# A four-layer graph kernel on one core: later places for a feature sum and for the gates' products, and a last row tile in two column halves

## The chip, the cores and the metric

The kernel runs on one core of one Trainium2 chip. The metric is the device time of one execution in microseconds; the time before is 2896.17 us, the median of three runs (2895.42 to 2900.82). A run with the hardware profiler gives, beside its own time, a record of each instruction: its engine, its start, its duration and the semaphores it waited for. The engines are called as the profile calls them: PE is TensorE's matrix product, PEld its loads of the stationary operand, DVE is VectorE, ACT is ScalarE, POOL is GpSimd, and SP is SyncE, which issues most loads.

## The reference, cut to what matters

There are 2708 nodes with 512 features, and an adjacency of 2708 x 2708, all in fp32. Each of four layers computes a new feature matrix, adds it to the old one and normalizes the rows.

```python
deg = jnp.maximum((adj != 0).astype(jnp.float32).sum(-1), 1.0)
x = _layernorm(x + _L0_gnn_ref(x, adj), axis=-1)
x = _layernorm(x + _L1_gnn_ref(x, adj, adj, ...), axis=-1)      # attention and two gates
x = _layernorm(x + _L2_gnn_ref(x, adj, L2_gnn_weight), axis=-1) # three hops, p = adj @ p
x = _layernorm(x + _L3_gnn_ref(x, adj, deg[..., None], L3_gnn_W, L3_gnn_b), axis=-1)

# layer 1, the gates
type_sum_a = adj_a @ x
type_sum_b = adj_b @ x
attn_a = sigmoid(concatenate([type_sum_a, x], axis=1) @ Wa.T + ba)
attn_b = sigmoid(concatenate([type_sum_b, x], axis=1) @ Wb.T + bb)
# ...
return sigmoid(attn_a * x_a + attn_b * x_b)

# layer 3, the last
a_norm = dinv * (adjacency + eye(n)) * dinv                     # dinv = node_degree ** -0.5
pooled = a_norm @ x + x
return relu(pooled @ W + b)
```

Here `node_degree` is the same shape as a column, so that the kernel can put both factors into one reciprocal per row and a diagonal that it adds to the adjacency.

## The kernel before

The kernel doesn't write its instructions in the order of the program. It collects functions in a list, each with a position, sorts the list and calls them; within one engine the recorded order then follows the list closely, though not exactly, since a scheduler has the last word. So a larger number in `at(...)` is a later place in the queues of the engines, and nothing else.

```python
    def at(pos, fn, hold=False):
        # ...
        events.append((pos, len(events), go if hold else fn))

    S = [28.0 * s for s in range(8)]          # where each sweep over the adjacency starts
    # ...
    for p, _, fn in sorted(events, key=lambda e: e[:2]):
        fn()
```

Products of large matrices are split into seven smaller ones by sums of quarter blocks (the scheme of Strassen and Winograd). Layer 1 has one level of it: per range of up to 384 rows there are seven sub-products of ten row tiles each, one list unit for each sub-product. Its results lie in C, whose halves are h = 1 and h = 0. From C come the gates: `pg` is four products of C with the padded gate weights, ScalarE copies it to `zg`, and `pz` takes from it two columns per row tile.

```python
    def done1(p0, dp, last, R0, n, h, C, tiles):
        Z = {}

        def gates():

            pg = bank("pg")
            for c in range(DC):
                nc.tensor.matmul(pg[32 * c : 32 * c + 32, :n], wab_pad[:, c, :], C[h, c][:, :n], start=True, stop=True)
            Z[0] = trans("zg")
            nc.scalar.copy(Z[0][:, :n], pg[:, :n])

        def gate_tile(i, t, lo, w):
            # ... pz<-pick,zg on TensorE, a sum on VectorE, a sigmoid on ScalarE

        at(p0 + 0.05, gates)
        for i, (t, lo, w) in enumerate(tiles):
            def b(i=i, t=t, lo=lo, w=w):
                gate_tile(i, t, lo, w)
                if not last:
                    return
                # ... last range: the dense product of this row tile, ps_d
            at(p0 + 0.25 + (dp * i if last else 0.02 * i), b)
        if last or h:
            return

        Y = {}
        at(p0 + 0.3, lambda: Y.update(row_sums({(i, c): C[1 - i, c] for i in range(2) for c in range(DC)}, n)))
        # ... seven(...) from p0 + 0.6 on: the dense products (ps) of these sums
```

`row_sums` writes some of its sums in place, over halves of C that `pg` reads. The degrees of the nodes are counted on the way: VectorE adds masks in `deg` (L974), and `ds` (L988) sums it by columns with 128x1 products. The scores of the attention are VectorE's work too (L911).

Layer 3, like the hops, has two levels. A range g has seven outer products, two list units each, and each outer product seven sub-products, `u = 2 / 7` units each. The moving operands `z` are blocks of the adjacency, loaded and combined in place (L1231) or corrected on the diagonal (L1245); the stationary ones are blocks `b11` to `b22` of the features and four sums of them, `t1` to `t4` (L1265).

```python
                def tsum(nm, x, y, T=T, st=st, nk=nk):
                    for i in range(2):
                        # ...
                        T[nm, i] = ring_tile("t")
                        nc.vector.tensor_tensor(get(nm), get(x), get(y), ALU.subtract)

                for nm, x, y, pos in (("t3", "b22", "b12", -0.9), ("t1", "b12", "b11", 0.1), ("t2", "b22", "t1", 0.9),
                                      ("t4", "b21", "t2", 1.9)):
                    if g == j == 0:
                        pos = max(pos, 0.4)
                    at(b + u * pos, lambda a=(nm, x, y), f=tsum: f(*a))
                # ...
                for i, (v, z, home, start) in enumerate((
                        ("b11", (0, 0), "u", 1), ("t3", "s3", "c", 1), ("t1", (1, 0), "d", 1), ("t2", (0, 0), "u", 0),
                        ("t4", (1, 1), "c", 0), ("b22", (0, 0), "d", 0), ("b21", (0, 1), "a", 1))):
                    for k in range(nk):
                        at(b + u * (i + k / nk), lambda a=(i, v, z, home, start, k), f=step: f(*a))
```

So `t3` of outer product j stands 0.9 of a sub-product ahead of it, and is first read by its second sub-product. In layer 3 the feature blocks B11 (group tiles B11A to B11D) come from the rows X3 that layer 2 writes just before; they serve the third outer product, j = 2 of g = 0.

The end of the kernel is six row tiles, of 128, 128, 83, 128, 128 and 83 rows, each finished by itself:

```python
            def b(s=s, lo=lo, w=w, r0=r0, got=got):
                px = dense(lambda c: cc(s, c)[:, lo : lo + w], W[6], w)
                r = 12 * g + 6 * h + 3 * s + lo // P
                nc.vector.scalar_tensor_tensor(px[:w], px[:w], rdeg_f[:w, r : r + 1], vec[6][:w], ALU.mult, ALU.add)
                finish(s, lo, w, got["x"], px)

            p = p0 - 0.095 + 0.14 * i
            at(p - 0.6, a)
            at(p, b)
```

`dense` is four products with all 512 columns, into one PSUM bank. `finish` takes the relu and adds the old row (L1491), lets `layernorm` compute the statistics (L557, L559, L561 on VectorE, a power of -1/2 on GpSimd at L562, L564 on VectorE), normalizes the 512 columns on ScalarE (L567) and stores the tile. The four steps after the product follow each other, each waiting for the one before.

Of the kernel before, what the change touches and what calls it, by code (L numbers as in the profile page):

```python
# [21 lines left out]
F32 = mybir.dt.float32  # L22
BF = mybir.dt.bfloat16
AF = mybir.ActivationFunctionType
ALU = mybir.AluOpType
P = 128
EPS = 1e-5
NH = 1354
# [40 lines left out]
def gnn_kernel(ctx: ExitStack, tc: tile.TileContext, x, adjT, w_sa, a_sa, w_gcn, b_gcn, wab, bab, w_hop, w_out,  # L69
               b_out, out):  # L70
    nc = tc.nc
    N, D = x.shape
    NT = 2 * KT
    DC = D // P
    HD = D // 2
# [94 lines left out]
    def bank(nm, shape=None):  # L170
        return psum.tile(shape or [P, D], F32, name=nm, tag="x", bufs=8)
# [6 lines left out]
    def at(pos, fn, hold=False):  # L178

        def go():  # L180
            n = len(nc.cur_bb.bb.instructions)
            fn()
            held.update(range(n, len(nc.cur_bb.bb.instructions)))

        events.append((pos, len(events), go if hold else fn))
# [819 lines left out]
# [12 lines that stand above are left out]
            if i == 0:  # L1017
                Z[1] = bank("pz", [P, 8])
            pz = Z[1][:, 2 * i : 2 * i + 2]
            nc.tensor.matmul(pz[:w], Z[0][:, lo : lo + w], pick, start=i == 0, stop=True, skip_group_check=True)  # L1020
            nc.vector.tensor_tensor(gate[:w, t, :], pz[:w], gate_x[:w, t, :], ALU.add)
            nc.scalar.activation(gate[:w, t, :], gate[:w, t, :], AF.Sigmoid)

        def finish(t, w, y):
            nc.scalar.mul(y[:w], y[:w], gate[:w, t, 1:2])
            move(nc.gpsimd, XB[t], y[:w])

        at(p0 + 0.05, gates)
        for i, (t, lo, w) in enumerate(tiles):
            def b(i=i, t=t, lo=lo, w=w):  # L1030
                gate_tile(i, t, lo, w)
                if not last:
                    return
                px = dense(lambda c: C[h, c][:, lo : lo + w], W[1], w)
                y = nat("y")
                nc.vector.tensor_tensor(y[:w], px[:w], vec[1][:w], ALU.add)
                finish(t, w, y)

            at(p0 + 0.25 + (dp * i if last else 0.02 * i), b)
        if last or h:  # L1040
            return

# [3 lines that stand above are left out]
            H, y = {}, []  # L1046

            def b7(part, t=t, lo=lo, w=w, H=H, y=y):
                if part == 0:
                    y.extend(nat("y") for _ in range(2))  # L1050
                seven(part, Y, W[8], H, lo, w, y, None, [vec[1], vec[1]])
                if part == 1:
                    for j in range(2):
                        finish(t + KT * (1 - j), w, y[j])

            at(p0 + 0.6 + 0.56 * i, lambda f=b7: f(0))
            at(p0 + 0.6 + 0.56 * i + 0.26, lambda f=b7: f(1))
# [142 lines left out]
    def sweep2(base, ext, done, on_diag=False):  # L1200
        nk = K2 + ext
        u = 2 / 7
        for g, (i0, n) in enumerate(RANGES2):
            Q, C = {}, {}
            for j, m in enumerate(ORDER2[g]):
# [61 lines left out]
                for nm, x, y, pos in (("t3", "b22", "b12", -0.9), ("t1", "b12", "b11", 0.1), ("t2", "b22", "t1", 0.9),  # L1267
                                      ("t4", "b21", "t2", 1.9)):
                    if g == j == 0:
                        pos = max(pos, 0.4)  # L1270
                    at(b + u * pos, lambda a=(nm, x, y), f=tsum: f(*a))

                def stat(v, k, T=T, st=st):
# [212 lines left out]
    def done6(p0, dp, g, i0, n, h, cc, tiles):  # L1486
# [12 lines left out]
        for i, (s, lo, w) in enumerate(tiles[:3] if not end else ()):  # L1499
# [7 lines left out]
            def b(part, lo=lo, w=w, got=got, z=z, H=H, r=r):  # L1507
                if part == 0:
                    z.extend(nat("z") for _ in range(2))
                seven(part, Y, W[7], H, lo, w, z, [rdeg_f[:w, r + 3 * s : r + 3 * s + 1] for s in range(2)],  # L1510
                      [vec[6], vec[6]])
                if part == 1:
                    for s in range(2):
                        finish(s, lo, w, got[s], z[s])
# [5 lines left out]
        for i, (s, lo, w) in enumerate(tiles[3:] + tiles[:3] if end else ()):  # L1520
            got = {}
            r0 = i0 + s * n + lo

            def a(r0=r0, w=w, got=got):
                got["x"] = fetch2(X3, h, r0, w)

            def b(s=s, lo=lo, w=w, r0=r0, got=got):
                px = dense(lambda c: cc(s, c)[:, lo : lo + w], W[6], w)
                r = 12 * g + 6 * h + 3 * s + lo // P
                nc.vector.scalar_tensor_tensor(px[:w], px[:w], rdeg_f[:w, r : r + 1], vec[6][:w], ALU.mult, ALU.add)  # L1530
                finish(s, lo, w, got["x"], px)

            p = p0 - 0.095 + 0.14 * i
            at(p - 0.6, a)
            at(p, b)

    sweep2(S[6], 0, done6, True)

# [54 lines left out]
```

## Time and profile before

| | |
|---|---|
| time, median of 3 runs | 2896.17 us (2895.42 to 2900.82) |
| span of the profiled run | 2892.7 us, granted TensorE clock 0.996 |
| TensorE, matrix product | 2839.9 us busy, 98% |
| TensorE, weight loads | 1871.5 us, 65% |
| VectorE | 2269.3 us, 78% |
| ScalarE | 569.2 us, 20% |
| GpSimd | 618.2 us, 21% |
| moved between HBM and the core | 511.52 MB, 177 GB/s on average |

The busy time of an engine counts what it executes, not its waits. "Idle before" in a line is the time that the engine stood before that instruction, with what ended the wait. One fp32 product of the program shows as two records of TensorE; ends of neighbouring records overlap a little, so that a group's length is its span and not a sum. Layer 1 lies between about 435 and 890 us, the products of layer 3 from about 2485 us to the end.

### The profile page before, as it was taken

How to read it: one execution, taken by the hardware profiler on the slowest of the kernel's cores; microseconds unless marked ns; L12 is line 12 of the kernel's file. 1: busy time of each engine (PE TensorE's matmuls, PEld its weight loads, DVE VectorE, ACT ScalarE, POOL GpSimd, SP SyncE). 2: the span in 40 equal slices, each digit the busy share in tenths (PEclk: the TensorE clock that was granted, in tenths of full speed). 3: DMA queues.
4: the chain of work that ended last, by engine and by line, in shares of the span. 5: the costliest groups of instructions: out<-in, count | busy, mean ns of one | idle time of the engine just before them, and what ended most of it. 6: DMA issues, size and time to landing. Idle time of an engine off the chain costs nothing. (4 is left out here: it accounts for less than half of the span.)

```text
span 2892.7 us, 37709 instructions
## 1 busy us (share of the span) xinstructions
PE 2839.9 (98%) x10955; PEld 1871.5 (65%) x10955; DVE 2269.3 (78%) x5875; ACT 569.2 (20%) x1122; POOL 618.2 (21%) x1119
## 2 busy tenths in 40 slices
PE   7999999999999999999999999999999999999998
PEld 6655665657765656866666666666666666666665
DVE  6998698576748775775699787887878878799987
ACT  4554200101136554542100000000000100100001
POOL 0223223123320101122213133031330211501202
PEclk9999999999999999999999999999999999999999
DMA  7666466354544433565677767566675665754552
GB/s 231 201 199 187 134 203 221 116 174 144 178 148 125 123 117 98 154 196 158 192 206 232 214 193 242 172 203 200 197 238 172 189 195 173 236 161 145 175 142 90
DMA packets 373455, 511.52 MB, mean 177 GB/s; under 512 B 63722, under 2 KB 326628, under 8 KB 373248
## 3 DMA queue, kind: packets, MB, share of 16 engines
q1 hardware_dynamic: 307128, 372.01, 44.0%
q0 software_dynamic: 49536, 126.39, 12.8%
q10 hardware_dynamic: 16584, 10.71, 1.3%
q8 instruction: 87, 1.43, 0.2%
q14 instruction: 120, 0.98, 0.1%
HBM read 425.22 MB, written 83.67 MB: 176 GB/s over the span
## 5 line engine op out<-in xcount | busy, mean ns | idle before, releaser
L1231 DVE TENSOR_TENSOR z<-z 128x339 f32<-128x339 f32 (+1 forms) x966 | 453.9, 502 | 13.9 <-PE accu L1284 4.0
L1302 ACT COPY q<-accu 128x338 f32<-128x338 f32 (+1 forms) x84 | 34.5, 442 | 1006.6 <-PE accu L1284 907.1
L562 POOL TENSOR_TENSOR rstd<-rstd,neg_half 128x1 f32<-128x1 f32 (+3 forms) x92 | 58.9, 640 | 771.4 <-DVE rstd L561 519.7
L1284 PE MATMUL accc<-s,t 128*128 128x338 f32 (+1 forms) x644 | 198.2, 450 | 0.0
L1284 PE MATMUL accu<-z,t 128*128 128x338 f32 (+1 forms) x644 | 194.5, 449 | 2.3 <-DVE z L1231 2.3
L1284 PE MATMUL accc<-z,t 128*128 128x338 f32 (+1 forms) x644 | 194.9, 450 | 0.5 <-ACT q L1302 0.5
L1284 PE MATMUL accd<-z,t 128*128 128x338 f32 (+1 forms) x644 | 193.9, 448 | 0.6 <-DVE q L1366 0.6
L1417 POOL DMA_DIRECT2D Y<-y x192 | 104.8, 552 | 364.0 <-DVE y L1412 332.2
L405 DVE TENSOR_TENSOR a<-a,a 128x384 f32<-128x384 f32 (+2 forms) x330 | 160.9, 508 | 11.9 <-PE accu L460 11.3
L1284 PEld LDWEIGHTS accc<-z,t 128*128 128x128 f32 x644 | 122.9, 191 | 62.4 <-issue 2.1
L1284 PEld LDWEIGHTS accc<-s,t 128*128 128x128 f32 x644 | 120.9, 190 | 64.1 <-issue 7.5
L1284 PEld LDWEIGHTS accu<-z,t 128*128 128x128 f32 x644 | 121.7, 190 | 62.8 <-DVE z L1231 2.9
L1284 PEld LDWEIGHTS accd<-z,t 128*128 128x128 f32 x644 | 121.9, 190 | 60.5 <-DVE q L1366 1.5
L1231 DVE TENSOR_TENSOR s<-z 128x338 f32<-128x338 f32 (+1 forms) x322 | 149.5, 502 | 13.2 <-PE accc L1284 8.0
L1308 DVE TENSOR_TENSOR q<-q,accd 128x338 f32<-128x338 f32 (+1 forms) x112 | 55.9, 499 | 115.3 <-PE accd L1284 115.1
L1083 ACT ACTIVATE e<-row,neg_s 128x384 f32<-128x384 f32 (+5 forms) x176 | 100.4, 571 | 75.8 <-DVE e L1085 21.7
L1084 ACT ACTIVATE f<-row,neg_s 128x384 f32<-128x384 f32 (+5 forms) x176 | 99.9, 567 | 19.6 <-PE accc L460 6.3
L1085 DVE TENSOR_TENSOR e<-e,f 128x384 f32<-128x384 f32 (+5 forms) x176 | 87.0, 505 | 18.4 <-ACT f L1084 17.6
L974 DVE SCALAR_TENSOR_TENSOR deg<-a,deg 128x384 f32<-128x384 f32 (+2 forms) x152 | 74.8, 503 | 19.2 <-DMA a<-in_adjT 18.2
L408 POOL DMA_DIRECT2D As<-a x120 | 64.8, 543 | 86.2 <-DVE a L405 81.5
L1086 DVE SCALAR_TENSOR_TENSOR a<-a,e 128x384 f32<-128x384 f32 (+2 forms) x160 | 79.8, 506 | 3.9 <-DMA a<-in_adjT 1.9
L771 DVE SCALAR_TENSOR_TENSOR s<-a,row 128x384 f32<-128x384 f32 (+2 forms) x152 | 75.0, 505 | 6.0 <-ACT row L756 6.0
(681 smaller groups left out, 5960.4 us busy)
## 6 DMA issues: line engine op xcount, KB each, us to landing
z<-As SPq DMA_DIRECT2D x320, 169.5 KB
z<-As SPq DMA_DIRECT2D x320, 169.0 KB
a<-in_adjT SPq DMA_DIRECT2D x240, 192.0 KB
z<-in_adjT SPq DMA_DIRECT2D x240, 169.5 KB
z<-in_adjT SPq DMA_DIRECT2D x240, 169.0 KB
a<-in_adjT SPq DMA_DIRECT2D x120, 165.0 KB
a<-in_adjT SPq DMA_DIRECT2D x112, 128.0 KB
As<-a POOLq DMA_DIRECT2D x60, 192.0 KB, 4.2
```

What stands on the lines that cost most here:

```text
L405: nc.vector.tensor_tensor(A[r, dst, k][:, :n], A[r, a, k][:, :n], A[r, b, k][:, :n], op)
L408: nc.gpsimd.dma_start(out=SD[m][k * P : (k + 1) * P, R0 : R0 + n], in_=A[r, dst, k][:, :n])
L562: nc.gpsimd.tensor_tensor(rstd[:w, 1:2], rstd[:w, 0:1], neg_half[:w], ALU.pow)
L771: nc.vector.scalar_tensor_tensor(t[:w, :n], a[:w, :n], 0.0, row[R0, h][:w, :n], ALU.is_gt, ALU.mult)
L974: nc.vector.scalar_tensor_tensor(d[:w, :n], a[:w, :n], 0.0, d[:w, :n], ALU.not_equal, ALU.add)
L1083: nc.scalar.activation(e[:w, :n], row[R0, h][0][:w, :n], AF.Exp, bias=neg_s[:w, t : t + 1])
L1084: nc.scalar.activation(f[:w, :n], row[R0, h][1][:w, :n], AF.Exp, bias=neg_s01[:w, t : t + 1])
L1085: nc.vector.tensor_tensor(e[:w, :n], e[:w, :n], f[:w, :n], ALU.min)
L1086: nc.vector.scalar_tensor_tensor(a[:w, :n], a[:w, :n], 0.0, e[:w, :n], ALU.not_equal, ALU.mult)
L1231: nc.vector.tensor_tensor(d[:, :n], Z[x + (k,)][:, :n], Z[y + (k,)][:, :n], op)
L1284: nc.tensor.matmul(B[home][:, :n], stat(v, k), a[:, :n], start=bool(start and k == 0), stop=k == nk - 1, skip_group_check=True)
L1417: nc.gpsimd.dma_start(out=rows[:, :, f * P : (f + 1) * P], in_=o[32 * f : 32 * (f + 1), : m * P].rearrange("p (b d) -> p b d", d=P))
```

## The change

Three places change. The feature sum t3 of the third outer product of the last layer (g = 0, j = 2 at `S[6]`) stands at the start of that product, not 0.9 of a sub-product ahead of it, so that its tiles have more time to arrive. The gates of layer 1 and their row tiles stand 0.15 units later, so that the sums they read have more time to be made. And the very last row tile has a version of its own: its product, scaling, relu, residual and statistics are done in two halves of 256 columns, each in a bank of its own, with the two sets of statistics joined by one aggregation; then ScalarE normalizes one half and VectorE the other, at the same time. What is computed stays the same.

```diff
--- before.py
+++ after.py
@@ -1025,7 +1025,7 @@
             nc.scalar.mul(y[:w], y[:w], gate[:w, t, 1:2])
             move(nc.gpsimd, XB[t], y[:w])
 
-        at(p0 + 0.05, gates)
+        at(p0 + 0.2, gates)
         for i, (t, lo, w) in enumerate(tiles):
             def b(i=i, t=t, lo=lo, w=w):
                 gate_tile(i, t, lo, w)
@@ -1036,7 +1036,7 @@
                 nc.vector.tensor_tensor(y[:w], px[:w], vec[1][:w], ALU.add)
                 finish(t, w, y)
 
-            at(p0 + 0.25 + (dp * i if last else 0.02 * i), b)
+            at(p0 + 0.4 + (dp * i if last else 0.02 * i), b)
         if last or h:
             return
 
@@ -1268,6 +1268,8 @@
                                       ("t4", "b21", "t2", 1.9)):
                     if g == j == 0:
                         pos = max(pos, 0.4)
+                    if g == 0 and j == 2 and base == S[6]:
+                        pos = max(pos, 0.0)
                     at(b + u * pos, lambda a=(nm, x, y), f=tsum: f(*a))
 
                 def stat(v, k, T=T, st=st):
@@ -1524,6 +1526,31 @@
             def a(r0=r0, w=w, got=got):
                 got["x"] = fetch2(X3, h, r0, w)
 
+            def b_last(s=s, lo=lo, w=w, r0=r0, got=got):
+
+                r = 12 * g + 6 * h + 3 * s + lo // P
+                y = got["x"]
+                st = small.tile([P, 2, 6], F32, name="st2", bufs=1)
+                for e in range(2):
+                    q = slice(e * HD, (e + 1) * HD)
+                    px = bank("ps_d")
+                    for c in range(DC):
+                        nc.tensor.matmul(px[:w, q], cc(s, c)[:, lo : lo + w], W[6][c][:, q], start=c == 0,
+                                         stop=c == DC - 1, skip_group_check=True)
+                    nc.vector.scalar_tensor_tensor(px[:w, q], px[:w, q], rdeg_f[:w, r : r + 1], vec[6][:w, q], ALU.mult,
+                                                   ALU.add)
+                    nc.vector.scalar_tensor_tensor(y[:w, q], px[:w, q], 0.0, y[:w, q], ALU.max, ALU.add)
+                    nc.vector.bn_stats(st[:w, e, :], y[:w, q])
+                mv = small.tile([P, 2], F32, name="mv")
+                nc.vector.bn_aggr(mv[:w], st[:w])
+                rstd = small.tile([P, 2], F32, name="rstd")
+                nc.vector.tensor_scalar(rstd[:w, 0:1], mv[:w, 1:2], EPS, None, ALU.add)
+                nc.gpsimd.tensor_tensor(rstd[:w, 1:2], rstd[:w, 0:1], neg_half[:w], ALU.pow)
+                nc.vector.scalar_tensor_tensor(rstd[:w, 0:1], mv[:w, 0:1], -1.0, rstd[:w, 1:2], ALU.mult, ALU.mult)
+                nc.scalar.activation(y[:w, :HD], y[:w, :HD], AF.Identity, bias=rstd[:w, 0:1], scale=rstd[:w, 1:2])
+                nc.vector.tensor_scalar(y[:w, HD:], y[:w, HD:], mv[:w, 0:1], rstd[:w, 1:2], ALU.subtract, ALU.mult)
+                move(nc.sync, out[h * NH + r0 : h * NH + r0 + w, :], y[:w])
+
             def b(s=s, lo=lo, w=w, r0=r0, got=got):
                 px = dense(lambda c: cc(s, c)[:, lo : lo + w], W[6], w)
                 r = 12 * g + 6 * h + 3 * s + lo // P
@@ -1532,7 +1559,7 @@
 
             p = p0 - 0.095 + 0.14 * i
             at(p - 0.6, a)
-            at(p, b)
+            at(p, b if i < 5 else b_last)
 
     sweep2(S[6], 0, done6, True)
 
```

## The prediction

> **What bounds the kernel now.** I read the page first, for the share of each engine; then, since TensorE leads, the waits of TensorE alone, longest first; then the order of time around the longest waits of the second half of the span; last the end of the span.
>
> ```profile
> PE 2839.9 (98%) x10955; PEld 1871.5 (65%) x10955; DVE 2269.3 (78%) x5875; ACT 569.2 (20%) x1122; POOL 618.2 (21%) x1119
> ```
>
> TensorE works for 2839.9 of 2892.7 us, so 52.8 us of idle time is all that a change of order can win. The stretches of the span (busy time by window) place it: 20.9 us lie in the first 100 us, and 8.8 us after 2800 us are nearly all the close, which has no matmul left. TensorE's waits show what remains; the columns are who waited for whom, total us, times, longest us.
>
> ```profile
> PE accd L1284 <- DVE z L1231: 3.9, 5, 2.5
> PE pg L1012 <- DVE C L521: 2.9, 1, 2.9
> PE accu L1284 <- DVE z L1231: 2.3, 1, 2.3
> ```
>
> Three single waits, 2.92, 2.48 and 2.31 us, which the change touches. The first, on TensorE and then on VectorE (start us, duration us, engine, line, what; in brackets the idle time before it and what ended it):
>
> ```profile
> 732.42 1.99 PE L460 MATMUL accd<-a,B22A 128*128 128x256 f32 x8
> 737.33 1.08 PE L1012 MATMUL pg<-C,wab_pad 128*32 128x256 f32 x4 [2.92 <-DVE C L521]
> 739.08 1.13 PE L460 MATMUL accd<-a,B22A 128*128 128x256 f32 x4
> 740.04 0.50 PE L988 MATMUL ds<-ones_f,deg 128*128 128x1 f32 x4
> ```
> ```profile
> 736.87 0.41 DVE L521 TENSOR_TENSOR C<-U,accc 128x256 f32<-128x256 f32 x1
> 738.06 0.41 DVE L521 TENSOR_TENSOR W<-W,accu 128x256 f32<-128x256 f32 x1
> ```
>
> The gates' products pg need four sums C and W. VectorE came to them late, out of a long run of score instructions (L911) that ended at 736.35, while TensorE stood from 734.41. The products listed just after pg (L460, L988) need nothing from C.
>
> The other two, first VectorE, then TensorE:
>
> ```profile
> 2523.08 0.55 DVE L1265 TENSOR_TENSOR t<-B11C,B11A 128x384 f32<-128x384 f32 x1
> 2527.26 0.43 DVE L1265 TENSOR_TENSOR t<-B11D,B11B 128x256 f32<-128x256 f32 x1 [3.63 <-DMA B11D<-X]
> 2527.60 0.61 DVE L1245 SCALAR_TENSOR_TENSOR z<-ident,diag,z 128x128 f32<-128x128 f32 x2
> 2528.13 0.50 DVE L1308 TENSOR_TENSOR q<-q,accd 128x338 f32<-128x338 f32 x1
> 2528.54 0.50 DVE L1231 TENSOR_TENSOR z<-z 128x338 f32<-128x338 f32 x1
> ```
> ```profile
> 2529.10 2.25 PE L1284 MATMUL accd<-z,B21C 128*128 128x338 f32 x6 [2.48 <-DVE z L1231]
> 2547.87 1.76 PE L1284 MATMUL accu<-z,t 128*128 128x338 f32 x4 [2.31 <-DVE z L1231]
> ```
>
> VectorE sat 3.63 us at one feature sum whose tile B11D was still on its way from memory. Behind it stood the z that TensorE wanted from 2526.62. After 2527.26 VectorE shows no idle time until past 2548 us, so the second wait is the same lost time, seen a product later.
>
> [...]
>
> **Part one, the gates later (0.15 of a list unit, layer 1).** In the built order of the changed kernel, pg of this half stands behind two more row tiles of accd and the ds products. By the lines above a row tile of 128x256 (4 records) is 1.99/2, with the overlap of ends about 0.87 us, and ds, 740.04 to 740.41, is 0.37. So 0.87 + 0.37 + 0.87 = 2.1 us of work is done inside the 2.92 us. Its inputs are there: the last deg that ds reads was written by 724.2. TensorE then arrives at about 736.5 and still waits 0.8 us for C; pg, paced by VectorE, ends at 739.08 as before. Gain: 2.1 us. The seven other gate groups had no wait of TensorE and gain nothing.
>
> **Part two, the feature sum later.** The sum t3 of the third product moves from 0.9 of a sub-product ahead of it to its start. A sub-product is 10 records of a 338-column matmul, 2.85 us, so t3 moves by some 2.6 us of list; in the built order nine VectorE tile operations more stand ahead of it, with the five z among them. From 2523.08 VectorE does two diagonal updates (0.53), a first s (0.42), q (0.42), then z at 0.42 each (starts in a run of L1231 are 0.42 apart). The first z is there by 2524.9, the fifth by 2527, and TensorE wants them from 2526.62 on at 0.57 apart: no wait. Then t3 comes up near 2528, after the B11D that arrived at 2527.26: no wait either. The 3.63 us of VectorE are gone. TensorE gets 2.48 of them at once. The second wait: VectorE reaches its z 3.63 earlier, TensorE needs it 2.48 earlier, so 2.31 - (3.63 - 2.48) = 1.16 stays. Gain together 2.48 + 1.15 = 3.63 us. TensorE uses t3 only at 2538 - 2.5, some 6 us after it is made.
>
> **Part three, the last row tile in halves.** The end now:
>
> ```profile
> 2885.48 0.69 DVE L1491 SCALAR_TENSOR_TENSOR ld<-ps_d,ld 83x512 f32<-83x512 f32 x1
> 2886.20 0.69 DVE L557 BATCH_NORM_STATS2 st<-ld 83x6 f32<-83x512 f32 x1
> 2888.01 0.16 DVE L564 SCALAR_TENSOR_TENSOR rstd<-mv,rstd 83x1 f32<-83x1 f32 x1 [0.72 <-POOL rstd L562]
> 2888.25 0.81 ACT L567 ACTIVATE ld<-ld,rstd 83x512 f32<-83x512 f32 x1 [2.63 <-DVE rstd L564]
> 2889.09 0.34 SPq L151 DMA_DIRECT2D out<-ld  x1
> ```
>
> TensorE's work stays: 8 records of 0.43 us become 16 of 0.216 (12 such L647 records took 2.59). The first half's product is there at 2884.53 - 1.73 = 2882.8. VectorE is at the tile before it until 2883.43. A half costs 0.75 - 0.27, 0.69 - 0.27 and 0.69 - 0.27 us[...], 1.4 us with gaps. The built order puts the first half's three operations among the small ones of the tile before, whose rstd update then waits for GpSimd: from the start of L561 to that of L564 is now 0.88 us, and L561 slips from 2883.68 to about 2884.35, so L564 goes at 2885.2 and the second half can start at 2885.3, though its product is there at 2884.5. It ends its statistics near 2886.7; before it was 2886.89. So 0.2 us is won of the 1.2 us that the head start might give. ScalarE then does 256 columns[...], beside VectorE's other half, 0.2 less. Gain 0.4 us; the store behind it is unchanged.
>
> **Sum.** 2.1 + 3.6 + 0.4 = 6.1 us; 2896.17 - 6.1 = 2890.1 us, 0.2%.
>
> **Rivals.** (1) The wait of the gates only changes place. In layer 1 the sums that follow write P1c in place and must wait for pg: today VectorE waits 3.5 us in 3 places for it, and with pg two row tiles of 384 columns later (2.6 us) it would wait some 2.6 us more each time. If TensorE then ran into those sums, part one would be lost: 2892.2. Against it: in the first range the sums were ready by 552.1, at least 2 us ahead of their turn, and the built order has the score sums behind them to absorb the delay. (2) Part two gives only the direct 2.48, because VectorE meets another unfinished transfer or a busy accumulator in the run after 2523; the 2.31 stays and the total is 2891.3. For it: this run now starts 3.6 us earlier against the same loads. Against: the loads that it reads were issued by 2522, and the accumulators it adds had 4 us of slack. (3) The halves lengthen the end, if VectorE's per-instruction cost outweighs the head start: +0.4 in place of -0.4, 2890.9. (4) The moved list entries change the queues of ScalarE and VectorE around 835 to 895 us, where gates, exponentials and table loads alternate; a fresh wait of 2 to 3 us would leave 2893. The changed order lets ScalarE do some exponentials before the gate copy it idled 11.80 us for, which speaks against it.
>
> **Range and chances.** The three before runs spread over 5.4 us, as much as the whole gain. All parts well and a lucky run give 2887; rivals 1 and 4 with a middling run 2894.5. A change of 2% is 58 us; nothing in the trace offers or threatens that: faster 0.005, same 0.99, slower 0.005.
>
> **What would show it.** Right: pg after two more row tiles, its wait under 1 us; no wait of VectorE for B11D; accd without its 2.48, the later accu wait at about 1.2; the last ACTIVATE 83x256 near 0.6 us and the last store issued about 0.4 us sooner after TensorE's end. Wrong: a new TensorE wait over 1 us at ps (L647) in layer 1 or at 890 to 910 us, a VectorE stall for another load after the moved sum, or second-half statistics that end later than 2.4 us after TensorE.

## The result, and the profile after

The changed kernel took 2884.68 us (median of 4 runs, 2883.16 to 2886.27), the kernel before 2895.80 in the runs beside it: a ratio of 0.9961, 95% interval 0.9943 to 0.9978, or 11.1 us less. The prediction had 2890.1 us, 6.1 less, and a range down to 2887.0; the result lies below it. Later runs of the same two kernels put part of the difference down to the draw: over all 25 runs of the changed kernel and 143 of the kernel before that this study has, the medians are 2887.11 and 2894.47 us, 7.4 us apart (95% interval 6.4 to 9.3, by drawing from the runs again and again). So two things are to be explained: why the change is worth 7 to 8 us and not 6, and why four runs could show 11.

The line of the engines, from the page of the changed kernel:

```profile
PE 2836.5 (98%) x10963; PEld 1870.9 (65%) x10963; DVE 2270.4 (79%) x5879; ACT 569.2 (20%) x1122; POOL 618.6 (21%) x1119
```

The span fell by 8.2 us, from 2892.7 to 2884.5. TensorE's busy time was not expected to move, for its products are the same; it fell by 3.4 us, 2839.9 to 2836.5. The other 4.8 us are idle time. Two of the waits of TensorE in the changed kernel (who for whom; total us, times, longest us; L1286 is the line that was L1284 before):

```profile
PE accu L1286 <- DVE z L1231: 1.6, 1, 1.6
...
PE pg L1012 <- DVE gate_x L921: 1.3, 1, 1.3
```

The three long ones of before (2.9, 2.5, 2.3) have become 1.3, nothing and 1.6 (the longest wait of accd is now 0.96 us). First the gates, on TensorE (start, duration, engine, line, what, idle before):

```profile
734.09 1.11 PE L460 MATMUL accd<-a,B22B 128*128 128x256 f32 x4
736.46 0.99 PE L1012 MATMUL pg<-C,wab_pad 128*32 128x256 f32 x4 [1.26 <-DVE gate_x L921]
```

pg stands behind the rest of the tiles of B22A, ds and a first tile of B22B, two row tiles later, as predicted, and its wait is 1.26 us. Then the last layer's third product on TensorE:

```profile
2540.78 1.40 PE L1286 MATMUL accu<-z,t 128*128 128x338 f32 x4 [1.58 <-DVE z L1231]
2542.02 3.01 PE L1286 MATMUL accc<-z,t 128*128 128x338 f32 x10
...
2547.27 1.12 PE L1286 MATMUL accd<-z,B11C 128*128 128x338 f32 x3 [0.54 <-DVE z L1231]
```

The wait of 2.48 us before accd<-z,B21C is gone. The second stays at 1.58, and 0.54 has come behind it. Last the end of the span, VectorE and then ScalarE:

```profile
2879.79 0.15 DVE L1549 SCALAR_TENSOR_TENSOR rstd<-mv,rstd 83x1 f32<-83x1 f32 x1 [0.72 <-POOL rstd L1548]
```
```profile
2880.03 0.60 ACT L1550 ACTIVATE ld<-ld,rstd 83x256 f32<-83x256 f32 x1 [1.80 <-DVE rstd L1549]
```

From TensorE's last product to the end of the span it was 8.17 us and is 7.87. The last row tile's store was issued 4.55 us behind that product before and 4.05 after, so 0.5 us sooner, but the end came only 0.3 sooner. What lies between is the close. GpSimd's DRAIN, which follows its last power, takes 4503 ns in both kernels, first before and then after (duration in ns min/median/max, first and last start):

```profile
L1589 POOLq DRAIN x3: 46/106/4503, 2887.4 to 2892.4; - x3
```
```profile
L1616 POOLq DRAIN x3: 46/106/4503, 2879.2 to 2884.2; - x3
```

The long one is the first. It starts 0.3 us sooner against TensorE's last product (2.87 us behind it before, 2.58 after), and the span ends 0.8 us behind its end in both. So the close followed the statistics, and what the normalization by two engines gained did not reach the end.

**What the prediction had not seen.** The four records behind the second wait (2.31 us) took 1.76 us in the kernel before. The ten that follow them:

```profile
2549.43 4.38 PE L1284 MATMUL accc<-z,t 128*128 128x338 f32 x10
```

4.38 us for ten records; after, the same ten take 3.01. The busy time by window says why. Columns: window, its length, busy us (and records) of PE, PEld, DVE, ACT, POOL, then PEclk, the granted clock of TensorE, then the share and GB/s of the DMA. Before:

```profile
2544.00:2548.78 4.78, 2.47 (x9) 1.41 (x8) 4.78 (x9) 0.00 (x0) 0.00 (x0) 1.00 0.47 128
2548.78:2552.19 3.41, 3.41 (x7) 2.02 (x6) 3.41 (x8) 0.78 (x2) 0.00 (x0) 0.50 0.58 173
```

Behind the wait the clock is 0.50 for 3.41 us, 7 records where 12 would fit (at 1.00 they start 0.284 us apart), and after it 1.00 again. In the profile before, there are five such stretches between the start-up (26 us) and the close, all on one grid of 3.413 us, from 84.35, 91.18, 435.93, 592.94 and 2548.78 us, each behind a window in which TensorE stood for 1.8 to 2.3 us; in the profile after there are three, from 84.09, 90.92 and 435.67. Two stretches at 1.7 us (half of 3.41) would be the 3.4 us of busy time.

The two longer waits of before halved nothing. On the same grid, the windows of the wait of 2.92 us at pg and of that of 2.48 us at accd:

```profile
732.89:736.30 3.41, 1.52 (x8) 0.99 (x6) 3.20 (x16) 0.89 (x1) 1.64 (x4) 1.00 0.32 86
736.30:739.71 3.41, 2.38 (x11) 1.13 (x12) 2.59 (x16) 1.13 (x4) 1.06 (x2) 1.00 0.77 221
2524.88:2528.30 3.42, 1.75 (x7) 0.83 (x5) 1.04 (x4) 0.00 (x0) 3.42 (x7) 1.00 0.69 195
2528.30:2531.71 3.41, 2.60 (x8) 1.44 (x9) 3.41 (x9) 0.00 (x0) 3.41 (x8) 1.00 0.90 253
```

Each of them lies across the border of two windows, with 1.89 and 1.03, and 1.67 and 0.81 us of idle time on the two sides. The wait of 2.31 us lay in one window whole.

So two theories, and a rival. **A**: a wait costs its own length and nothing else, which is what the prediction's sum took for granted. **B**: a wait of which some 2 us lie inside one window also halves the clock in the next, which costs up to another 1.7 us; the grid lies elsewhere in each of the two profiles (84.35 and 84.09 us), so the same wait may do this in one execution and not in another. **C**: the rest comes from the other order of the queues in the first layers.

### The profile page after: what moved, and what is told of

The parts are those of the page before. It is cut to its first block, busy times and chain, and to the rows that moved or that the text cites. A ratio compares the mean times of both kernels' runs of the same rounds, so it can differ in the third digit from the quotient of the medians.

```text
span 2884.5 us, 37727 instructions
## 1 busy us (share of the span) xinstructions
PE 2836.5 (98%) x10963; PEld 1870.9 (65%) x10963; DVE 2270.4 (79%) x5879; ACT 569.2 (20%) x1122; POOL 618.6 (21%) x1119
## 5 line engine op out<-in xcount | busy, mean ns | idle before, releaser
L1286 PE MATMUL accc<-s,t 128*128 128x338 f32 (+1 forms) x644 | 198.2, 450 | 0.0
L1286 PE MATMUL accu<-z,t 128*128 128x338 f32 (+1 forms) x644 | 194.0, 448 | 1.6 <-DVE z L1231 1.6
L1286 PE MATMUL accd<-z,t 128*128 128x338 f32 (+1 forms) x644 | 193.9, 448 | 0.6 <-DVE q L1368 0.6
L1286 PE MATMUL accc<-z,t 128*128 128x338 f32 (+1 forms) x644 | 193.5, 448 | 0.5 <-ACT q L1304 0.5
L1286 PEld LDWEIGHTS accc<-s,t 128*128 128x128 f32 x644 | 120.9, 190 | 64.1 <-issue 7.5
L1286 PEld LDWEIGHTS accc<-z,t 128*128 128x128 f32 x644 | 122.0, 190 | 61.6 <-issue 1.0
L1286 PEld LDWEIGHTS accu<-z,t 128*128 128x128 f32 x644 | 121.7, 190 | 61.9 <-DVE z L1231 2.1
L1286 PEld LDWEIGHTS accd<-z,t 128*128 128x128 f32 x644 | 121.9, 190 | 60.5 <-DVE q L1368 1.5
```

What stands on the lines that cost most here:

```text
L1286: nc.tensor.matmul(B[home][:, :n], stat(v, k), a[:, :n], start=bool(start and k == 0), stop=k == nk - 1, skip_group_check=True)
```

## Experiments

### The parts alone

The gates alone:

```diff
-        at(p0 + 0.05, gates)
+        at(p0 + 0.2, gates)
-            at(p0 + 0.25 + (dp * i if last else 0.02 * i), b)
+            at(p0 + 0.4 + (dp * i if last else 0.02 * i), b)
```

> Only the gates' products and the tiles behind them are listed later. Theory A (a wait costs its own length and nothing else): the wait before the gates at 734 us shrinks from 2.92 to 1.26 us, so 1.7 us less than the kernel before, and not more than 2.1. Theory B (a TensorE wait of some 2 us or more also halves the granted clock for one stretch of 3.4 us, in some executions and not in others, which costs 1.7 us each time): 1.7 us and about three quarters of another 1.7, so about 3.0 us less on the mean; TensorE's busy time in a profile differs by multiples of 1.7 us, with a PEclk of 0.5 behind the waits. Theory C (the gain beyond the waits comes from another order of the queues in the first two layers): more than 4 us less from this part alone.

Measured 2891.12 us beside 2894.52 (0.9988, 0.9981 to 0.9995): 3.4 us less. The wait at pg was 0.9 us in its profile. The interval, 1.4 to 5.5 us, holds what each of the three theories expects.

The sum alone:

```diff
                     if g == j == 0:
                         pos = max(pos, 0.4)
+                    if g == 0 and j == 2 and base == S[6]:
+                        pos = max(pos, 0.0)
```

> Only the feature sum t3 of the last layer's third product is listed later. Theory A: the wait of 2.48 us at 2526 us goes, and of the wait of 2.31 us at 2545 about 0.2 goes (1.58 and 0.54 stay): 2.7 us less, at most 3.1. Theory B: also the two stretches of halved clock which those two waits draw in about six executions of ten each, 2 x 0.6 x 1.7 = 2.0 us: about 4.7 us less. In the profile the products of t2 and t4 behind the second wait take 1.30 and 3.00 us, not 1.76 and 4.38. Theory C: less than 2.7 us, for the rest would come from the first two layers.

It took 2890.76 us (0.9987, 0.9980 to 0.9993): 3.8 us less, between theories A and B, and with an interval of 2.0 to 5.8 us that holds both.

The last tile alone (with `b_last` as in the change), and then the other two parts without it:

```diff
-            at(p, b)
+            at(p, b if i < 5 else b_last)
```

> Only the very last row tile is done in two halves of its columns. All theories: the work behind TensorE's last product gets shorter by about 0.25 to 0.4 us, and nothing else moves; no difference that the runs can tell from zero (0 to 1 us less).

It took 2894.77 us (1.0002, 0.9994 to 1.0011): no difference by the time.

> Gates and sum later, the last tile as before: the whole change without its third part. Theory A: 1.7 + 2.7 = 4.4 us less than before. Theory B: 3.0 + 4.7 = 7.7 us less, the sum of the two parts alone within a microsecond or so. Theory C: not the sum of the two parts. Beside the whole change (11.1 us less by its median, 8.2 by the two profiles) this should be 0.25 to 0.4 us longer.

It took 2886.18 us (0.9971, 0.9959 to 0.9982): 8.3 us less, where the two parts alone add to 7.2. The interval, 5.2 to 11.9 us, leaves out A's 4.4. The intervals allow the whole to be the sum of the parts, so nothing calls for C, though the times don't rule it out.

One time per run doesn't separate the parts, for the runs of one kernel spread over 10 us. The traces do: each was cut at the same four products, and the length of each part set beside the number of halved stretches in it (in brackets).

| kernel | pr at 91 us to P1c at 434 | rcol at 592 to the last layer's first transposes at 2490 (holds the gates) | from there to T3C at 2625 (holds the sum) | T3C to the end (holds the halves) |
|---|---|---|---|---|
| before | 343.7 (1) | 1899.4 (1) | 141.3 (1) | 259.6 |
| gates alone | 341.6 (0) | 1894.5 (0) | 140.9 (1) | 259.7 |
| sum alone | 344.1 (1.6) | 1898.7 (0) | 136.5 (0) | 259.7 |
| halves alone | 342.1 (0) | 1900.0 (1) | 140.8 (1) | 259.4 |
| gates and sum | 344.1 (1.5) | 1894.9 (0) | 136.5 (0) | 259.7 |
| after | 343.7 (1) | 1896.1 (0) | 136.5 (0) | 259.4 |

The first column holds nothing of the change and shows the price of a halved stretch: over all profiles without fills, 341.6 to 342.1 us without one, 343.1 to 344.1 with one. The second holds the gates, but other waits too, so that its single profiles scatter; the gates are cut out more closely below. The third shows the sum: 4.3 to 4.8 us, of which one stretch. The last shows the halves: 0.3 us, in each kernel that has them.

### Filling the waits with useless products

If idle time halves the clock, products that nobody reads, put into the wait, must keep it up. Four of the waits can take them without another engine's order changing.

```diff
+    junk = const.tile([P, 256], BF, name="junk")
+    nc.vector.memset(junk, 1.0)
...
+    def fill(o, times, start=True):
+        # products that nobody reads, for the time in which TensorE would wait
+        def go():
+            for _ in range(times):
+                nc.tensor.matmul(o[:, :256], ones_bf, junk, start=start, stop=True, skip_group_check=True)
+
+        keep(go)
...
         pr = bank("pr")
+        if (R0, h) == (0, 0):
+            fill(pr, 12)
```

`keep` holds them at their place in the list. Likewise there are 18 before the count at 81 us, 22 before pg and 12 before ps_n at 2490.

> The kernel before, with products added that nobody reads (bfloat16, 128x256, about 0.1 us each) in four of TensorE's waits: 18 in the one of 2.02 us at 81 us, 12 in that of 1.83 at 89, 22 in that of 2.92 at 734, 12 in that of 1.84 at 2490. No wait ends earlier, and the other engines keep their order; TensorE gets 64 products, some 6.8 us, more to do. Theory A (a wait costs its own length and nothing else): the same time as before, or up to 1 us longer where a fill runs over. Theory B (a wait of some 2 us inside one stretch of the clock halves the granted clock for the next 3.4 us, 1.7 us lost): the first three of these waits each halve it in somewhat over half of the executions, so about two stretches fewer on the mean, 3 to 3.5 us less time, the mean granted clock up by 0.001 from 0.9972, and no PEclk below 1 behind these four waits in the profile. Theory C says nothing of this one.

It took 2892.60 us beside 2894.01 (0.9994, 0.9986 to 1.0002): 1.4 us less, not 3 to 3.5, and by the interval perhaps nothing. In its profile 18 of the products take 2.13 us and 12 take 1.47, so 0.11 us for each more. It has none of the stretches behind the four waits, and the granted clock rose as B expected, from 0.9970 on the mean of 39 runs to 0.9981 on that of 13. But B's price was wrong, and the traces show where. The kernel before, with the clock halved from 84.35 us:

```profile
84.41 2.05 PE L469 MATMUL accc<-aw,B21B 128*128 128x256 f32 x4
...
91.09 0.85 PE L753 MATMUL pr<-ident,r 128*128 128x128 f32 x3 [1.83 <-DVE r L745]
```

The kernel with the sum alone, whose clock stayed whole there:

```profile
84.48 1.11 PE L469 MATMUL accc<-aw,B21B 128*128 128x256 f32 x4
...
91.19 0.90 PE L753 MATMUL pr<-ident,r 128*128 128x128 f32 x3 [2.75 <-DVE r L745]
```

pr starts at the same time. What the whole clock wins at 84 us is waited away at 89, since pr waits for VectorE's r and not for TensorE. A halved stretch ahead of a wait on another engine cost nothing here. That leaves the stretches behind 89 us (in eleven of the fifteen profiles without a fill there) and 734 us (in two of seven with the long wait), 1.7 us in all on the mean at most, and what a fill costs where it runs over.

> As the filled kernel before, with fewer products: 6, 5, 12 and 4 in the four waits, so that about 1.4, 1.3, 1.6 and 1.4 us of each stay idle. Theory A: the same time as before. Theory B, with a limit of 1.7 to 2.1 us of idle time inside one stretch, as the profiles so far have it: the same gain as with the full fills, 3 to 3.5 us. If any wait over a microsecond halved the clock, half fills would gain nothing.

It took 2894.30 us (1.0001, 0.9993 to 1.0010): nothing gained, though its profile has no stretch behind the four waits either. With an effect of 1.7 us this pair of runs can't tell the theories apart.

The same fills in the changed kernel, and one of them alone:

> The changed kernel with products that nobody reads in the waits that it has left and that can take them: 18 at 81 us, 12 at 89, 7 at 735, 12 at 2487. Theory A: the time of the changed kernel. Theory B: the stretches behind the waits at 81 and 89 us go, 1.2 stretches on the mean: about 2 us less than the changed kernel, and faster than both.

It took 2888.86 us beside 2894.01 (0.9981, 0.9974 to 0.9988), slower than the changed kernel, by 2.4 us against its runs of the same time (2886.50) and by 1.8 against all 25. This goes against what B expected. Seven products before pg, 0.77 us by the 0.11 above, are as long as the wait often is: 0 to 0.9 us in most later profiles of the changed kernel. The rest of the loss lies between pg and the last layer's first transposes (1754.9 us, against 1751.5 to 1752.6 in profiles of the changed kernel without the fills) and was not traced to a cause.

> The changed kernel with one fill alone: 12 products that nobody reads (1.3 us) in the wait at 89 us, which is 1.8 to 2.75 us long and halves the clock in about six profiles of ten. The fill at 81 us is left out: it made the counts that the wait at 89 is for come later, and the halved clock behind 81 us lies before that wait, which absorbs it. Theory A: the time of the changed kernel. Theory B: 1 us less, about 2885.5 where the changed kernel has 2886.5: hardly to be told apart by its time, but the segment from 91 to 434 us in its profile takes 341.6 to 342.1 us, not 343.1 to 344.1.

It took 2886.76 us beside 2893.72 (0.9975, 0.9964 to 0.9986): the time of the changed kernel. Its first part took 341.8 us, with no stretch, as B has it, but the gain of 1 us doesn't show in the time.

### Ten waits of known length

The clean test is a stage without waits, with a clock of 1.00 throughout, into which waits are put. A chain runs from TensorE over nine ScalarE copies back to TensorE, ten times in the fifth sweep, with TensorE's order kept around it; the second kernel also has ten useless products in each wait, the third has four copies instead of nine. In the code these are `range(10)` for `range(0)`, and `range(3)` for `range(8)`.

```diff
+    def stall(o):
+        # ...
+        w = wab_pad.rearrange("p c d -> p (c d)")
+        # ...
+        nc.tensor.matmul(o[:, :P], ident, ident, start=True, stop=True, skip_group_check=True)
+        nc.scalar.copy(w, o[:, :P])
+        for _ in range(8):
+            nc.scalar.copy(w, w)
+        for _ in range(0):
+            nc.tensor.matmul(o[:, :P], ident, ident, start=True, stop=True, skip_group_check=True)
+        nc.tensor.matmul(o[:, :P], ident, w, start=True, stop=True, skip_group_check=True)
+        # ...
...
+                    if base == S[4] and j in (1, 2, 3, 4, 5) and (i, k) == (5, 0):
+                        B["a"] = bank("acca")
+                        stall(B["a"])
```

> The kernel before, with ten waits of known making added in a stage in which TensorE never waits and PEclk is 1.00 throughout (the fifth of the seven sweeps): a product, nine ScalarE copies of it one after the other, and a product of the last copy, which TensorE has to wait for; its order is kept around them. Each wait should be 2.5 to 3 us, by nine copies of 128x128 at some 0.25 us and the ways there and back. Theory A: the time grows by ten times the wait and the two small products, 30 us if a wait is 2.7. Theory B: each wait also halves the clock for 3.4 us in six or seven cases of ten, so 1.1 us more for each: 40 us and more, the mean granted clock lower by 0.004, and PEclk 0.5 behind most of the ten.

It took 2947.93 us beside 2893.72 (1.0183, 1.0161 to 1.0204): 54.2 us more, with a mean clock of 0.991. Its four runs lie far apart, from 2936.79 to 2955.79 us.

> The same ten chains, with ten products that nobody reads (float32, 128x128, about 0.21 us each) behind each first product, so that some 2.1 us of each wait are filled and the chain ends when it did. Every other instruction stands as in the kernel with the ten waits. Theory A: the same time as that kernel. Theory B: no halved clock behind the ten, so about 11 us less than that kernel, though TensorE has 100 products more to do, and the clock as in the kernel before.

It took 2933.61 us (1.0139, 1.0123 to 1.0154), with a clock of 0.997: 14.3 us less than with the bare waits, with 100 products more to do.

> The same ten chains with four copies in place of nine, so waits of about 1.3 to 1.5 us. Theory A: the time grows over that of the kernel before by ten times this wait and the two small products, some 18 us. Theory B with its limit (1.7 to 2.1 us of idle time inside one stretch): also some 18 us, the clock not lower than before. If every wait halved the clock, it would be 30 us and more.

It took 2914.87 us (1.0073, 1.0060 to 1.0086), with a clock between 0.996 and 0.998: 21.2 us more than before.

One of the ten places on TensorE. With the bare wait:

```profile
1827.54 0.49 PE L200 MATMUL acca<-wab_pad,ident 128*128 128x128 f32 x2 [3.04 <-ACT wab_pad L197]
1827.86 2.71 PE L1304 MATMUL accd<-z,B11C 128*128 128x338 f32 x6
```

With the wait filled:

```profile
1827.24 0.49 PE L200 MATMUL acca<-wab_pad,ident 128*128 128x128 f32 x2
1827.57 1.87 PE L1304 MATMUL accd<-z,B11C 128*128 128x338 f32 x6
```

With the short wait:

```profile
1824.77 0.49 PE L200 MATMUL acca<-wab_pad,ident 128*128 128x128 f32 x2 [1.40 <-ACT wab_pad L197]
1825.09 1.87 PE L1304 MATMUL accd<-z,B11C 128*128 128x338 f32 x6
```

From the chain's first product to its last it is 3.43 us, filled or not; the nine copies take 2.87 us of it (the first 0.27, the other eight 2.60), and the ten useless products 2.50. But the group behind it takes 2.71 us after the bare wait (and the next one 2.76), 1.87 each after the filled and the short one: 1.7 us lost. The windows around the bare wait, on the grid of that run:

```profile
1825.34:1828.75 3.41, 1.21 (x6) 0.93 (x7) 2.73 (x7) 1.95 (x7) 0.00 (x0) 1.00 0.60 201
1828.75:1832.16 3.41, 3.41 (x8) 2.05 (x7) 2.31 (x5) 0.00 (x0) 0.00 (x0) 0.50 0.01 3
```

TensorE was busy 1.21 of 3.41 us, and the next window has half the clock; the one after it is at 1.00 again. All ten bare waits of 3.0 us did this in the profile (twelve halved stretches, two of the ten having two); none of the filled and none of the 1.40 us waits did. It was ten of ten by their place too: the larger part of each in one window was 1.98 to 2.59 us, and a wait of 3.0 us could also lie half in one window and half in the next. From the short waits to the long ones the wait grew by 10 x 1.65 = 16.5 us and the time by 33.1, and by 19.4 even from the slowest of the short runs to the fastest of the long ones. A is refuted. The other half goes with the halved stretches, and most of it, 14.3 us, goes away where useless products are all that is added.

### The wait that stayed

First the change once more, beside new runs of the kernel before:

> The whole change, as it stands, beside the same runs of the kernel before as the filled ones. By the parts alone (medians 3.4 and 3.8 us less, the last tile nothing) 7.2 us less; the kernel without the third part had 8.3 less. Theory A: 4.5 to 5 us less. Theory B: 7 to 9 us less, and the 11.1 of the first four runs was partly their luck with the clock.

It took 2886.50 us beside 2894.01 (0.9972, 0.9961 to 0.9984): 7.5 us less by the medians.

One wait was still to be explained. The second wait of the sum was to shrink to 1.16 us and kept 1.58 and 0.54. On VectorE, in the changed kernel, the four sums of a weight group (T1C from 2535.53 us, then T2C, T3C, T4C) stand ahead of the z that TensorE wants:

```profile
2538.56 0.94 DVE L357 TENSOR_TENSOR T4C<-B21C,T2C 128x768 f32<-128x768 f32 x1
...
2540.23 0.91 DVE L1231 TENSOR_TENSOR z<-z 128x338 f32<-128x338 f32 x2
```

T4C isn't read before 2626 us. So these sums were moved, for three of the four groups:

```diff
-            at(base + 4.2 + 0.3 * i, lambda g=g: sums(g), True)
+            at(base + 4.2 + 0.3 * i + (0.4 if i and base == S[6] else 0), lambda g=g: sums(g), True)
```

> The changed kernel, and in the last layer the sums T1 to T4 of the weight groups C, B and D also listed later, behind the z of the third product. If VectorE's queue is what makes TensorE wait there: the waits of 1.58 us (2539) and 0.54 us (2547) go, the stretch from TensorE's first transposes of the last layer at 2489 us to its feature product at 2615 takes 124.7 us in place of 126.8, and the time is 2.1 us below that of the changed kernel beside it; the wait is too short to halve the clock, so theories A and B expect the same. If the wait has another cause, or comes back where the sums now stand: the same time as the changed kernel.

This kernel took 2886.88 us beside 2894.60 (0.9972, 0.9960 to 0.9983). The changed kernel of the same runs:

> The changed kernel again. Theory A (waits alone, 4.5 us by the idle times of the two profiles; 6.1 by the prediction): 4.5 to 6 us below the kernel before. Theory B: 7 to 8, of which some 5.5 are the waits and the rest stretches of halved clock that are not drawn in.

It took 2887.16 us (0.9971, 0.9961 to 0.9982), so the later sums gained 0.3 us by the medians, not 2.1. Both waits are gone from their profile, and the stage from 2490 us to T3C took 136.1 us against 136.6 of the changed kernel. The idle time fell by 1.9 us and came back as busy time. In the changed kernel:

```profile
2557.20 0.85 PE L1361 MATMUL accr<-r,B22R 32*128 32x338 f32 x8
```

With the later sums:

```profile
2552.90 0.83 PE L1361 MATMUL accr<-r,B22R 32*128 32x338 f32 x2
2553.66 0.83 PE L1286 MATMUL accu<-z,T2A 128*128 128x338 f32 x2
...
2555.96 0.84 PE L1361 MATMUL accr<-r,B22R 32*128 32x338 f32 x4
```

Four products of 32 rows, eight records, take 0.85 us, as long as two such records alone (0.83). They overlap: in the first profile of the changed kernel four records start 7 ns apart at 2555.55 us and four at 2555.94, where full ones start 284 ns apart. Torn apart by full products into three pieces, from 2552.90, 2554.43 and 2555.96 us, they take three such times: 1.5 us lost. The two full products between them take 0.77 us each from start to start, where 0.57 is usual: another 0.4, together the 1.9.

> The kernel before with those sums of C, B and D later, and the sum t3 where it was. The first wait (2.48 us at 2526) stays, for they stand behind it; the second (2.31 at 2545) goes. Theory A: 2.3 us below the kernel before. Theory B: 2.3 and, in about six executions of ten, another 1.7 for the stretch that the second wait halves: 3.3 us less.

It took 2892.82 us (0.9996, 0.9990 to 1.0003): 1.8 us less by the medians, not told from zero. The second wait went; the first is there, and others came (a third of 0.73 us at 2566.96):

```profile
2529.28 2.25 PE L1284 MATMUL accd<-z,B21C 128*128 128x338 f32 x6 [2.54 <-DVE z L1231]
...
2551.27 0.84 PE L1284 MATMUL accd<-z,B11C 128*128 128x338 f32 x2 [0.99 <-DVE z L1231]
```

With 0.3 in place of 0.4 the 32-row products stay together:

> The changed kernel with the sums T1 to T4 of C, B and D later by 0.3 units, not 0.4: TensorE's list keeps the four 32-row products of B22R one behind the other. If their being torn apart is what ate the gain: the stage from 2489 us to the first product of T3C at 2625, 136.5 us in the changed kernel and 136.1 with 0.4 units, takes 134.6, and the whole 1.9 us less than the changed kernel, about 2884.7. If VectorE's full queue gives the wait back elsewhere: 136 again, and the time of the changed kernel.

It took 2885.52 us beside 2894.93 (0.9968, 0.9956 to 0.9981). The changed kernel of the same runs:

> The changed kernel, beside the one with the later sums: 7 to 8.5 us below the kernel before, by the ten and the seven runs so far, and its stage from 2489 us to T3C 136.5 us.

It took 2888.24 us (0.9974, 0.9963 to 0.9984). The two intervals overlap, and the stage that the edit touches is not shorter with the sums 0.3 later: 137.5 us, against 136.7. The waits are back under other names:

```profile
2542.35 1.68 PE L1286 MATMUL accd<-z,B11C 128*128 128x338 f32 x4 [1.69 <-DVE z L1231]
...
2549.18 1.40 PE L1286 MATMUL accu<-z,T2A 128*128 128x338 f32 x4 [1.18 <-DVE z L1245]
```

VectorE shows no idle time between 2530 and 2570 us in the changed kernel (20.00 of 20.00 us busy):

```profile
2530.00:2550.00 20.00, 17.84 (x63) 11.27 (x61) 20.00 (x37) 1.67 (x4) 1.06 (x2) 1.00 0.69 200
2550.00:2570.00 20.00, 20.00 (x81) 12.47 (x80) 20.00 (x54) 0.00 (x0) 0.00 (x0) 1.00 0.61 172
```

In three orders of these sums the stage thus took 136.6, 136.1 and 137.5 us. While VectorE's queue was full, what one wait gave up came back as another wait or as torn products; that no order could do better isn't shown. No version tried is shown to be faster than the change.

## Why the prediction was wrong, step by step

- **Gates, 2.1 us.** The mechanism held: pg stands behind two more row tiles, and TensorE gave nothing back later. As its first rival feared, VectorE's wait for pg in the first range grew, from 1.4 to 4.4 us, but TensorE's waits at ps (L647) are 1.3 us in 3 places before and after; the fourth rival didn't come either. In seven profiles without this part the wait was 1.8 to 2.9 us, 2.3 on the mean; in nine with it 0 to 1.3, 0.6 on the mean: 1.7 us. By length it is a little more. From one product of accd<-a,T1A at 700.1 us to one of accd<-a,B22C at 745.0 (times of the profile before, the same two in every kernel) the seven took 44.8 us on the mean of the five without a halved stretch, the nine 42.8: 2.0 us. The profile puts the wait that is left down to gate_x. pg doesn't read it, and the first C was done 0.15 us before pg began, so what ended that wait isn't settled.
- **Sum, 2.48 + 1.15 us.** The 2.48 held, with no stall for B11D. Of the 1.15 only 0.2 came as waits, for 2.31 us became 1.58 and 0.54: the step "VectorE reaches its z 3.63 earlier" took the time that VectorE no longer stood as free for that z, and other work stood ahead of it. The idle time of the stage fell by 2.7 us (5.4 to 2.7), not 3.6. Its length, though, fell by 3.4 where no halved stretch is in it (139.8 and 140.0 with fills elsewhere, 136.5 after), close to the 3.63. Part of the difference is that this wait cost more than its listed idle time: at the wait of 2.48 us two products start 2.92 us apart where 0.28 is usual, which is 2.64 more, and the first product takes 0.55 us in place of 0.45. So the near hit of 3.63 is partly luck.
- **Halves, 0.4 us.** It was 0.3, and the ACTIVATE took 0.60 us, near the 0.6 expected. The 0.27 us that a half was to save on each VectorE step, and the 0.2 on ScalarE, were the author's estimates; after, 256 columns on VectorE take 0.47, 0.42 and 0.42 us where 512 in the tile before take 0.75, 0.69 and 0.70. But the 0.4 was 0.2 for the statistics and 0.2 for ScalarE, with the store behind it unchanged, and that missed what ends the kernel: the store came 0.5 us sooner, while the end followed GpSimd's DRAIN, which only the statistics bring forward, by 0.3. That 0.3 and 0.4 are near is luck.
- **Sum of the steps.** This is the step that failed: "2.1 + 3.6 + 0.4 = 6.1 us" counts each wait by its length alone, and takes TensorE's busy time as fixed. One of the two waits of the sum's stage, or their like, halved the clock in six of eight profiles with the sum where it was, and in none of ten with it later: the stage took 141.0 us at the median with a halved stretch and 139.9 in the two profiles without, so 1.1 us for it, some 0.8 on the mean. The wait at pg did it in two of seven, with 45.4 and 46.9 us in place of 44.8, 0.4 us on the mean. With these, 2.0 + 3.4 + 0.3 + 0.8 + 0.4 = 6.9 us, within the 6.4 to 9.3 that all runs give; the 6.1 is just outside. Each run's granted clock agrees: it is 0.9978 on the mean of the 25 runs of the changed kernel and 0.9971 on that of 139 runs of the kernel before, and one halved stretch lowers it by 0.0006 (half of 3.413 in 2890 us). The step could have been taken from the profile before, which had "1.76" for four records after the wait, quoted in the prediction, against 1.30 for four without it.
- **Level and range.** The result lies 5.4 us below the predicted 2890.1: 1.7 us because 2896.17 was the median of three runs and 143 have 2894.47, 1.3 because the effect is 7.4 us and not 6.1, and 2.4 because the first four runs of the changed kernel drew 2884.68 where 25 have 2887.11. The prediction named a spread of 5.4 us and then set the lower end by "a lucky run" without knowing what the luck is. In part it is the clock: over 139 runs of the kernel before, time and mean granted clock go against each other with a correlation of -0.57, 1.8 us for 0.001; the rest of the spread has no cause here. The profile before had two stretches more than the profile after. The one behind 2545 us is the change's doing; that behind 590 us is not shown to be, since the wait there halved the clock in two later profiles of the changed kernel too.

## What to carry to other kernels

In these traces a wait of TensorE cost its length plus, where some 2 us of it fell inside one window of 3.4 us, a halved window behind it, up to 1.7 us. Whether they fell so changed from execution to execution (six of eight profiles at the sum's stage, two of seven at pg), so this part is to be priced as a share of 1.7. And it counts only if TensorE's speed matters there: ahead of the wait for r at 89 us the loss was absorbed, with pr at 91.09 us after a halved stretch and at 91.19 without. So remove waits over 2 us first, or cut them to 1.5: no window with less than 1.66 us of idle time was followed by a halved one. Where the engine that TensorE waits for has a full queue, measure the length of the whole stage and don't add up single waits.

## What the runs showed of the hardware

- The clock was halved for a whole window of 3.413 us after a window at full clock in which TensorE stood long enough. Laid on this grid, the 19 profiles have, between start-up and close, 15739 full-clock windows with less than 1.66 us of idle time, and none was followed by a halved one. All 29 with 2.06 us or more were. Of the 59 between, 31 were; what decides there stays open.
- Fills with products that nobody reads kept the clock up: 0.997 against 0.991 with fp32 products, which cost nothing in chains that took 3.43 us with or without them. Behind the four waits filled with bfloat16 products there were no halved stretches either, but these fills gained no time that the runs can tell from zero, and the changed kernel with four of them was slower.
- Four 32-row products took 0.85 us in a row, and 0.83 to 0.84 us each time they were met singly or in a pair between full products.
- GpSimd's DRAIN at the end took 4.50 us, and the span ended 0.8 us after it in both kernels, although the last store had moved by 0.5 us against TensorE's end.
